# A new order of all operations, after the list scheduler's costs for the first products and the first loads are changed

## The chip, the cores and the metric

The kernel runs on one core of one Trainium2 chip. The metric is the device time of one execution in microseconds. The core has five engines with a queue of instructions each: TensorE (PE, matrix products), VectorE (DVE), ScalarE (ACT), GpSimd (POOL) and SyncE (SP), which here issues the transfers (DMA). An engine takes its instructions in the order in which the program lists them and waits where an input or a buffer isn't ready.

## The reference

The input `u` has 2 sequences of 2048 rows of 512 numbers. One block of a network is computed, with two parts.

- The mixer: `u @ W_in^T` gives z (1024 columns), xBC (1152) and 8 step sizes. xBC goes through a causal convolution of length 4 and `silu`, and is split into x (8 heads of 128), B and C (64 each). A state space scan follows for each head: within a chunk a masked product of C, B and decay factors with x, across chunks a carried state. The result is gated with `silu(z)`, normalised by its root mean square and multiplied with `W_out^T`. `u` is added, and each row is normalised to mean 0 and variance 1.
- The feed-forward part: the three weights are rounded to -1, 0, 1 times their mean magnitude. `hidden = silu(x @ wu^T) * (x @ wg^T)` has 2048 columns, and `hidden @ wd^T` is added to x; each row is normalised again.

## The kernel before

**Tiling.** The mixer works through 16 groups `g` of 256 rows, each of two chunks `c` of 128. The feed-forward part works through 8 blocks `b` of 512 rows. It computes its products by a scheme with seven instead of eight (P1 to P7 of `pair` and `down`), in 8 pairs `p` of blocks of hidden columns.

**Precision.** Operands of the large products are split into a high and a low float16 part. So weights are scaled first: `wsplit` loads a piece of a weight, squares and sums it on ACT (`sq`), sums over the partitions with a product (`mm`), takes a root on GpSimd (`pw`), and then writes the high part (`hi`, ACT) and the low part (`lo`, DVE). The window of `u` that a group needs goes the same way in `proj`: `ul` (L657) loads it, `usq` squares it, `usmm` sums, then come `uh` (ACT, L730 to L732) and `ulo` (DVE, L733).

**Names of steps.** In `proj`, `z{c}{j}` are products for z (L757), `x{j}` products for xBC (L774), each 12 instructions; `xt{j}` transposes (L789). `steps` makes the decay factors, `scan` the chunk's products (`yo`, `st`, `yd`) and the output products `o0` to `o2` (L974). In `pair`, `FP1.3` is product P1 of pair 3 (L1087); in `down`, `FQP20` is product P2 for one half of the rows (L1139), and `FRc11` and the like (L1149) add its bank to the residual. After the last `down` come row statistics, a root on GpSimd, the scaling and the output (L1235 to L1254).

**The order.** The program is not written in the order in which it runs. Each step is recorded as an operation with an engine, a cost in microseconds, the tiles it reads and writes and, for a transfer, its size `kb`. Then `Order.run` (L417) plays a list scheduler: it advances a clock, and whenever an engine is free it starts the operation with the lowest key whose inputs are done and whose buffers can be had. Buffers are handed out in the same pass. The resulting sequence is the program, and the time of the scheduler's clock is used for nothing else. The keys are the table `KEYS` (L41), one number for each of the 6287 operations in the order of their recording, in tenths of a microsecond; a small number is urgent. In the scheduler, a transfer ends `kb * 1.024 / BW` after the transfer before it or after its own start, with `BW = 290.0` (L368).

**The head.** The kernel's first loads are weights for `wsplit` (L645), the first window of `u` (L657) and the output weight in 8 pieces, twice (L685 and L702). While they come, PE has 80 groups of 4 products of a constant that nobody reads (L710 to L714, `WARM = 80`). They stand in the same list with keys of their own, and so are put between the real products.

```python
        for n in range(WARM):
            def idle():
                for i in range(4):
                    T.matmul(warm[:, :P * 2], oh[:, :P], oh, start=True, stop=True)
            op("", "PE", 4 * 0.109, idle, w=[warm], lat=0.0)
```

Of the kernel before, what the change touches and what calls it, by code (L numbers as in the profile page):

```python
# [41 lines left out]
69 16 66 80 87 90 97 100 115 245 279 287 327 330 338 340 348 165 176 219 233 273 283 290 292 314 46 89 100 114 123  # L42
131 134 152 112 155 166 188 191 198 201 212 136 179 191 207 217 224 229 241 191 240 276 283 302 309 313 358 305 355
383 403 479 532 548 563 347 392 192 263 272 514 530 748 759 773 798 725 753 765 771 226 260 299 333 337 371 361 395
238 272 292 326 351 385 220 254 406 412 895 929 936 782 817 826 944 978 990 863 897 915 923 957 984 902 936 976 998
1045 1071 788 822 838 24 28 32 37 41 46 50 54 59 63 67 72 76 83 87 92 96 103 107 112 116 120 127 131 136 140 145 149
153 158 162 169 173 207 212 216 220 225 229 236 254 272 279 283 307 312 316 334 338 343 350 354 374 379 401 408 412
436 441 445 450 492 496 503 534 546 550 554 561 603 608 645 650 681 693 697 701 706 743 748 113 125 132 135 142 144
164 259 750 820 343 374 397 194 265 278 417 473 470 290 345 350 482 484 541 502 509 515 520 522 524 526 528 530 533
536 542 546 555 562 579 592 662 595 636 680 691 660 621 664 672 649 361 381 393 399 404 440 444 448 539 547 385 402  # L50
408 437 453 543 559 597 507 530 537 543 551 636 643 686 194 215 229 237 253 368 399 426 178 196 208 225 233 285 358
378 320 346 354 375 380 493 500 534 240 267 274 279 285 392 434 485 476 499 505 510 515 594 601 639 258 288 300 305
310 481 490 496 872 924 821 852 726 753 841 866 303 347 379 390 398 429 441 868 486 531 626 660 662 458 503 488 663
700 834 1011 903 787 846 793 800 811 821 825 833 844 847 858 865 872 879 890 897 902 904 922 924 968 1003 1052 1062
1032 993 1044 1037 1021 521 539 547 556 579 669 677 664 690 721 565 602 610 615 621 717 724 746 772 810 816 821 834
908 929 991 612 631 639 644 649 742 752 782 654 681 687 700 705 802 810 831 668 696 710 715 720 768 786 805 759 788
794 801 812 872 889 921 710 748 755 761 767 828 838 882 858 885 891 898 904 988 1010 1066 931 963 584 606 909 942
949 984 454 534 724 781 787 797 859 738 805 812 952 727 775 788 958 967 983 987 994 1008 1021 1070 1053 1079 1114
1204 1357 541 560 845 944 946 966 873 866 891 1114 880 998 1012 1101 848 1004 1070 1107 1123 1138 1147 1155 1167
1230 1271 1211 1254 1315 1399 1500 911 926 934 937 944 947 964 1043 1010 997 1021 1060 1118 993 1015 1016 1070 1077  # L60
1266 1106 1225 1385 1412 1388 1390 1392 1394 1396 1398 1400 1402 1404 1406 1408 1410 1412 1414 1417 1424 1457 1524
1466 1505 1554 1564 1510 1491 1534 1546 1534 1145 1176 1182 1187 1192 1230 1280 1276 1251 1265 1101 1133 1139 1149
1160 1184 1195 1247 1173 1190 1196 1212 1222 1261 1271 1292 1333 1359 1366 1372 1377 1382 1387 1435 1237 1276 1286
1291 1296 1342 1346 1363 979 1005 1011 1017 1033 1069 1096 1149 1302 1330 1336 1351 1361 1366 1371 1379 1198 1220
1226 1242 1259 1289 1300 1339 1039 1072 1085 1090 1096 1151 1158 1187 1585 1627 1664 1684 1547 1583 1730 1766 686
751 1138 1113 1124 1132 1153 1143 1160 1263 1164 1176 1187 1279 1200 1216 1229 1305 1320 1335 1341 1348 1362 1433
1446 1406 1458 1491 1560 1868 754 895 1300 1258 1273 1287 1447 1462 1533 1623 1340 1355 1362 1478 1315 1329 1348
1472 1486 1498 1501 1508 1521 1748 1761 1567 1628 1806 1915 2034 1086 1098 1191 1203 1211 1234 1246 1733 1414 1290
1511 1562 1569 1389 1422 1423 1572 1574 1675 1650 1771 1604 1621 1620 1622 1634 1636 1652 1657 1673 1680 1686 1694
1701 1716 1721 1736 1743 1748 1787 1786 1873 1927 1978 1970 1952 1907 1950 1988 1963 1478 1519 1525 1530 1542 1553  # L70
1640 1627 1565 1762 1792 1822 1828 1833 1839 1974 2004 2027 1602 1631 1637 1653 1658 1805 1836 1933 1694 1716 1722
1737 1744 1930 1940 1993 1373 1412 1418 1424 1429 1438 1442 1471 1444 1481 1488 1493 1499 1504 1508 1541 1429 1446
1453 1459 1468 1538 1545 1557 1273 1295 1301 1311 1325 1442 1475 1501 1650 1689 1695 1702 1717 1763 1770 1819 1753
1786 1772 1826 1879 1936 1838 1873 1528 1634 1600 1657 1674 1681 1603 1609 1616 1811 1662 1687 1721 1798 1641 1680
1712 1792 1808 1838 1855 1862 1878 1936 1986 1923 1973 2034 2076 2332 1357 1415 1693 1791 1804 1823 1929 1996 2006
2052 1726 1862 1870 1958 1706 1889 1896 1964 1982 2002 2005 2013 2039 2264 2277 2083 2244 2322 2375 2471 1776 1790
1810 1820 1827 1831 1843 1999 1935 1876 1956 1986 1978 1905 1948 1950 1995 2003 2267 2035 2226 2297 2368 2304 2311
2313 2315 2318 2320 2325 2330 2339 2344 2360 2367 2369 2371 2373 2377 2390 2459 2396 2429 2481 2488 2458 2422 2473
2465 2447 1942 1995 2003 2008 2013 2023 2103 2107 2052 2111 1856 1879 1885 1895 1900 2000 2032 2040 2125 2144 2150
2155 2160 2363 2399 2415 1990 2030 2038 2043 2048 2108 2114 2256 2277 2314 2321 2326 2331 2348 2352 2395 2019 2068  # L80
2074 2079 2085 2241 2261 2286 2101 2121 2128 2138 2143 2298 2306 2345 2057 2082 2089 2103 2113 2283 2290 2301 2339
2370 2377 2382 2392 2435 2467 2483 2567 2608 2165 2207 2148 2183 2195 2221 1646 1699 2084 2047 2063 2070 2170 2176
2183 2251 2093 2107 2116 2233 2117 2132 2139 2239 2304 2316 2318 2326 2337 2400 2434 2382 2450 2489 2513 2821 1708
1741 2291 2232 2245 2264 2416 2422 2435 2576 2293 2305 2313 2428 2349 2361 2368 2434 2441 2454 2456 2464 2476 2560
2636 2520 2550 2681 2864 2975 2042 2054 2168 2178 2186 2188 2200 2574 2231 2230 2227 2262 2263 2402 2457 2457 2460
2498 2705 2581 2598 2665 2765 2676 2681 2715 2717 2729 2736 2748 2755 2758 2760 2762 2764 2766 2771 2776 2782 2811
2846 2815 2860 2903 2911 2870 2840 2883 2891 2881 2650 2680 2686 2694 2710 2806 2838 2834 2822 2862 2213 2258 2277
2282 2287 2367 2419 2439 2616 2666 2677 2682 2690 2859 2869 2884 2292 2321 2335 2340 2345 2432 2447 2461 2421 2452
2461 2496 2502 2591 2598 2606 2585 2613 2624 2634 2644 2671 2679 2803 2355 2380 2386 2396 2412 2480 2487 2594 2474
2533 2539 2544 2552 2646 2663 2674 2507 2542 2548 2556 2572 2603 2614 2659 2765 2799 2924 3000 2729 2756 2698 2723  # L90
2308 2374 2522 2587 2590 2601 2530 2524 2538 2648 2606 2628 2641 2781 2596 2617 2632 2658 2788 2805 2807 2815 2826
2862 2896 2871 2906 2941 3018 3232 2469 2588 2716 2623 2638 2666 2847 2840 2856 2969 2737 2748 2756 2825 2718 2730
2747 2819 2935 2947 2950 2957 2980 3157 3171 3025 3127 3216 3271 3355 2618 2629 2671 2674 2681 2686 2698 3025 2808
2758 2805 2835 2832 2787 2817 2810 2874 2921 2984 2971 2976 3094 3204 3115 3169 3174 3180 3187 3189 3191 3194 3197
3199 3201 3203 3205 3207 3209 3211 3251 3290 3254 3280 3335 3323 3319 3301 3346 3358 3330 2891 2931 2943 2948 2953
2993 3009 3004 3004 3052 2958 3005 3012 3018 3028 3038 3056 3088 3099 3143 3149 3170 3175 3283 3304 3364 3042 3064
3073 3079 3089 3109 3125 3210 3007 3042 3048 3054 3069 3090 3096 3117 2716 2761 2767 2772 2777 2881 2888 2900 2838
2873 2879 2899 2918 2968 2989 2997 2825 2847 2853 2858 2875 2897 2904 2981 3083 3113 3123 3133 3153 3213 3233 3256
3180 3221 3488 3547 3371 3408 3337 3380 2852 2981 2952 2980 2984 2991 2963 2957 2972 3093 3001 3032 3071 3181 2990
# [416 lines left out]
def mamba_ffn_kernel(  # L516
# [5 lines left out]
    nc = tc.nc  # L522
# [43 lines left out]
    with ExitStack() as ph:  # L566
# [4 lines left out]
        op = od.op  # L571
# [71 lines left out]
        def wsplit(nm, part, slot, src, dst, lo, n, tag):  # L643
            st = mk(tag, [P, n])
# [10 lines left out]
        def load_u(g):  # L655
            raw = uraws[g] = mk("uraw", [P, 4, TW])
            op("ul", "SP", 0.5, lambda: nc.sync.dma_start(out=raw.ap, in_=uT[g]), w=[raw], kb=520)  # L657
# [25 lines left out]
        for n in range(8):  # L683
            raw = mk("fraw", [P, DM])
# [15 lines left out]
        for n in range(8):  # L700
            raw = mk("fraw", [P, DM])
# [601 lines left out]
```

## Time and profile before

| what | us |
|---|---|
| median of 3 runs | 1363.52 (1363.44 to 1363.9) |
| the profiled execution | 1363.4 |
| its span, first to last instruction | 1361.7 |
| TensorE busy with products | 1347.8 |
| VectorE, ScalarE, GpSimd busy | 1162.3, 1067.4, 85.3 |
| first product begins, last one ends | 1.1, 1354.0 |

The profile is of one execution. Its span is 1.7 us shorter than the time of that execution. A product's end is modelled: products are pipelined, so in a run of products each is shown longer than the distance to the next. Mixer work fills the stretch from the start to about 800 us, feed-forward work what follows; the head is the part with unread products, up to 77 us. In the rows of waits the columns are the waiting engine with its tile and line, what it waited for, the total in us, the times, and the longest.

### The profile page before, as it was taken

The numbers are of one execution on the slowest core, as the hardware profiler recorded it, in microseconds if no ns is written. First come the engines' busy times: TensorE is split into PE (matmuls) and PEld (weight loads), VectorE is DVE, ScalarE is ACT, GpSimd is POOL, SyncE is SP. The second block draws the span as 40 slices with busy tenths as digits, with TensorE's granted clock in tenths as the row PEclk, the third lists the DMA queues.
The fourth block names the chain that finished last, engine by engine and source line by source line (L and its number), as shares of the span: only waits on it lengthen the run. The fifth ranks groups of instructions, "written<-read, shape, count | busy, mean of one in ns | idle before, by whom it ended". The sixth has DMA issues, their size and how long they took to land.

```text
span 1361.7 us, 29015 instructions
## 1 busy us (share of the span) xinstructions
PE 1347.8 (99%) x11046; PEld 1061.1 (78%) x11046; DVE 1162.3 (85%) x3111; ACT 1067.4 (78%) x2015; POOL 85.3 (6%) x128
## 2 busy tenths in 40 slices
PE   9999999999999999999999999999999999999997
PEld 8877676666767676776666688888888888888886
DVE  5789869988988889999998787988979697979885
ACT  7888878787877878879877785969788686969663
POOL 1000000000000000000000100001010101010000
PEclk9999999999999999999999999999999999999999
DMA  6434553564525625446559721313232232322001
GB/s 219 142 95 124 146 142 97 160 170 132 147 57 140 173 63 148 141 141 158 124 139 218 191 52 26 92 40 102 48 91 50 86 55 94 48 85 49 24 17 47
DMA packets 194811, 145.60 MB, mean 107 GB/s; under 512 B 140656, under 2 KB 151920, under 8 KB 194672
## 3 DMA queue, kind: packets, MB, share of 16 engines
q1 hardware_dynamic: 194672, 143.75, 40.3%
q8 instruction: 86, 1.41, 0.4%
q14 instruction: 53, 0.43, 0.1%
HBM read 89.84 MB, written 22.41 MB: 82 GB/s over the span
## 4 chain that ended last, share of the span: by engine, by line
PE 74%; DVE 13%; ACT 8%; DMA 4%; issue 1%; POOL 0%; SPq 0%; POOLq 0%; ACTq 0%; DVEq 0%
PE sd L1087 13%; PE mm L757 8%; PE po L974 8%; PE mm L774 7%; PE sd L1139 6%; PE po L1087 5%; PE mm L1087 5%; DVE acc L781 3%; PE ms L1087 3%; PE po L1139 3%; PE sd L954 3%; PE mm L1139 3%; PE tr L1087 2%; PE tr L789 1%; PE sd L917 1%
## 5 line engine op out<-in xcount | busy, mean ns | idle before, releaser
L781 DVE SCALAR_TENSOR_TENSOR acc<-mm,cwu,acc 128x256 f32<-128x256 f32 x432 | 202.7, 481 | 21.0 <-ACT acc L779 18.5
L1087 PEld LDWEIGHTS <-wx 128*128 128x128 fp8e4 x2048 | 200.3, 98 | 24.2
L774 PEld LDWEIGHTS <-wx 128*128 128x128 f16 x1728 | 165.6, 97 | 36.7 <-issue 3.6
L1087 PEld LDWEIGHTS <-wz 128*128 128x128 fp8e4 x1536 | 150.3, 98 | 18.2
L774 PE MATMUL mm<-uh,wx 128*128 128x260 f16 x1152 | 152.4, 274 | 1.6 <-DVE v L762 0.7
L757 PE MATMUL mm<-wz,uh 128*128 128x344 f16 x768 | 127.7, 309 | 1.1 <-ACT sz L764 0.5
L974 PE MATMUL po<-wo,th 128*128 128x512 f16 x512 | 121.1, 379 | 0.1
L779 ACT ACTIVATE acc<-mm,cst,cwu 128x256 f32<-128x256 f32 x144 | 80.1, 557 | 34.0 <-PE mm L774 33.6
L757 PEld LDWEIGHTS <-uh 128*128 128x128 f16 x768 | 74.0, 98 | 39.0 <-issue 3.8
L974 PEld LDWEIGHTS <-th 128*128 128x128 f16 x512 | 48.8, 98 | 49.7 <-issue 0.8
L774 PE MATMUL mm<-ul,wx 128*128 128x260 f16 x576 | 87.6, 273 | 0.0
L785 ACT ACTIVATE xc<-acc 128x256 f32<-128x256 f32 x128 | 52.6, 413 | 29.3 <-DVE acc L781 28.4
L757 PE MATMUL mm<-wz,ul 128*128 128x344 f16 x384 | 71.7, 309 | 0.0
L947 DVE SCALAR_TENSOR_TENSOR cr<-cr,dt,gm 128x128 f32<-128x128 f32 x256 | 71.4, 347 | 0.2
L764 ACT ACTIVATE sz<-mm,szs 128x344 f32<-128x344 f32 (+1 forms) x96 | 51.3, 538 | 21.3 <-PE mm L757 20.0
L954 PE MATMUL sd<-xt,cr 128*128 128x128 f32 x512 | 67.5, 278 | 0.0
L954 PEld LDWEIGHTS sd<-xt,cr 128*128 128x128 f32 x512 | 62.2, 192 | 3.3 <-DVE rr L834 0.4
L974 PE MATMUL po<-wo,tl 128*128 128x512 f16 x256 | 60.5, 379 | 0.0
L865 DVE TENSOR_SCALAR cr<-cr,cum 128x128 f32<-128x128 f32 x256 | 54.0, 282 | 5.2 <-DMA cr<-cum_scratch 5.2
L791 ACT ACTIVATE xt<-tr 128x256 f32<-128x256 f32 x128 | 48.1, 375 | 12.4 <-PE tr L789 12.3
L1139 PEld LDWEIGHTS <-xt 128*128 128x128 f16 x512 | 50.0, 98 | 7.2 <-DVE xt L1122 1.2
L757 PEld LDWEIGHTS <-ul 128*128 128x128 f16 x384 | 37.6, 98 | 18.4
(319 smaller groups left out, 3294.2 us busy)
## 6 DMA issues: line engine op xcount, KB each, us to landing
cr<-cum_scratch SPq DMA_DIRECT2D x32, 512.0 KB, 5.2
uraw<-in_uT_dram SPq DMA_DIRECT2D x16, 520.0 KB, 3.6
ec<-cum_scratch SPq DMA_DIRECT2D x64, 128.0 KB, 5.5
fraw<-in_wupT_dram SPq DMA_DIRECT2D x32, 256.0 KB, 3.4
s_scratch<-js SPq DMA_DIRECT2D x32, 256.0 KB, 2.7
x<-s_scratch SPq DMA_DIRECT2D x32, 256.0 KB, 3.0
fraw<-in_wgateT_dram SPq DMA_DIRECT2D x32, 256.0 KB, 3.5
fraw<-in_wdownT_dram SPq DMA_DIRECT2D x32, 256.0 KB, 3.0
```

What stands on the lines that cost most here:

```text
L757: T.matmul(ps[:, :ZC], (uh, ul)[a][:, k, HL + c * P:HL + (c + 1) * P], wz4[b]()[:, j, k, :], start=(n == 0), stop=(n == 11))
L764: op(f"sz{c}{j}", "S", act(w, 1), lambda: S.activation(d["sz"][c][:, j * ZC:j * ZC + w], ps[:, :w], AF.Silu, scale=szs[:, j:j + 1]), r=[ps ...
L774: T.matmul(ps[:, :TW], wx4[a]()[:, j, k, :], (uh, ul)[b][:, k, :], start=(n == 0), stop=(n == 11))
L779: op(f"t{j}3", "S", act(TG, 2), lambda: S.activation(acc.ap, ps[:, HL:TW], AF.Identity, bias=cb[:, j:j + 1], scale=cwu[:, j, 3:4]), r=[ps, ...
L781: op(f"t{j}{k}", "V", stt(TG), lambda k=k: V.scalar_tensor_tensor(acc.ap, ps[:, 1 + k:1 + k + TG], cwu[:, j, k:k + 1], acc.ap, ALU.mult, A ...
L785: op(f"xs{j}", "S", silu(TG), lambda: S.activation(xc.ap, acc.ap, AF.Silu), r=[acc], w=[xc], table="silu")
L865: V.tensor_scalar(cr[:, h, :], cr[:, h, :], cum[:, c * NH + h:c * NH + h + 1], 0.0, ALU.subtract, ALU.min)
L947: V.scalar_tensor_tensor(cr[:, h, :], cr[:, h, :], dt[:, c, h:h + 1], gm.ap, ALU.mult, ALU.mult)
L954: T.matmul(yp[hf][:, i * P:(i + 1) * P], cr[:, h, :], xt[:, c, h, :], start=is_first(g, c), stop=(is_first(g, c) or i == 3))
L974: T.matmul(po.ap, t[:, k, :], wo3[b]()[:, k, :], start=(q == 0 and k == 0), stop=(q == 2 and k == 7))
L1087: T.matmul(bank_[:, fi * TG:(fi + 1) * TG], wt[:, kt, f * P:(f + 1) * P], xT[i][:, a, :, kt, :], start=(first and fi == 0 and n == 0), sto ...
L1139: T.matmul(bank_[:, s_ * TG:(s_ + 1) * TG], X[k][j][:, a, e, s_ * P:(s_ + 1) * P], wt[:, k, :], start=(first and s_ == 0 and k == 0 and a ...
```

## The change

Five costs that the list scheduler uses are changed, and all 6287 keys. The instructions of the program are the same; their order on every queue, SP's and GpSimd's among them, and the choice of buffers follow from the new keys and costs.

- The transfers of the weight pieces, of the first window of `u` and of the output weight count as 0.72 of their former size (`n` columns of 128 rows of 4 bytes are n / 2 KB).
- The first 6 of the 80 groups of unread products count 0.213 us for each product instead of 0.109.

```diff
 KEYS = """
-69 16 66 80 87 90 97 100 115 245 279 287 327 330 338 340 348 165 176 219 233 273 283 290 292 314 46 89 100 114 123
...
-13492 13503 13508 13528 13474 13484 13499 13497 13504 13515 13533
+57 2 44 59 85 99 106 109 123 184 218 225 247 272 280 285 295 179 103 141 154 165 167 175 178 190 -6 32 43 56 63 71
...
-            op(nm + "ld", "SP", 0.5, lambda: nc.sync.dma_start(out=st.ap, in_=src[:, lo:lo + n]), w=[st], kb=n / 2)
+            op(nm + "ld", "SP", 0.5, lambda: nc.sync.dma_start(out=st.ap, in_=src[:, lo:lo + n]), w=[st], kb=0.36 * n)
...
-            op("ul", "SP", 0.5, lambda: nc.sync.dma_start(out=raw.ap, in_=uT[g]), w=[raw], kb=520)
+            op("ul", "SP", 0.5, lambda: nc.sync.dma_start(out=raw.ap, in_=uT[g]), w=[raw], kb=520 if g else 374)
...
-            op(f"wa{n}ld", "SP", 0.5, lambda n=n, raw=raw: nc.sync.dma_start(out=raw.ap, in_=woT[:, n, :]), w=[raw], kb=256)
+            op(f"wa{n}ld", "SP", 0.5, lambda n=n, raw=raw: nc.sync.dma_start(out=raw.ap, in_=woT[:, n, :]), w=[raw], kb=184)
...
-            op(f"wb{n}ld", "SP", 0.5, lambda n=n, raw=raw: nc.sync.dma_start(out=raw.ap, in_=woT[:, n, :]), w=[raw], kb=256)
+            op(f"wb{n}ld", "SP", 0.5, lambda n=n, raw=raw: nc.sync.dma_start(out=raw.ap, in_=woT[:, n, :]), w=[raw], kb=184)
...
-            op("", "PE", 4 * 0.109, idle, w=[warm], lat=0.0)
+            op("", "PE", 4 * (0.213 if n < 6 else 0.109), idle, w=[warm], lat=0.0)
```

The first number of the table is the key of the first load of `u`, and the second that of the load of wz2. The numbers of the 80 groups of unread products go from 2.4 to 74.8 us before, and from -2.3 to 93.0 after. The first loads by their new numbers are wx2 (-2.2), wx1 (-0.6), wz2 (0.2), wx3 (3.2), u (5.7), wx0 (10.3), wz1 (10.8), the constants (17.9), wx8 (18.4) and wz0 (25.9); before they were wz2 (1.6), wx1 (4.6), u (6.9), wx2 (11.2), wx3 (13.6), the constants (16.5), wx0 (17.6), wz0 (19.1), wx8 (24.5) and wz1 (30.5).

## The prediction

> **What bounds the kernel now.** I read the page first, for the share of each engine; then the busy times by stretch; then the waits of TensorE alone; then the head and the end of the timeline.
>
> ```profile
> span 1361.7 us, 29015 instructions
> PE 1347.8 (99%) x11046; PEld 1061.1 (78%) x11046; DVE 1162.3 (85%) x3111; ACT 1067.4 (78%) x2015; POOL 85.3 (6%) x128
> ```
>
> TensorE is the bound: 1361.7 - 1347.8 = 13.9 us of the span are not covered by a product. The stretches (columns: length, then busy us of PE, PEld, DVE, ACT, POOL, the granted clock, DMA share, GB/s) say where:
>
> ```profile
> 0.00:100.00 100.00, 98.22 (x810) 78.79 (x811) 72.67 (x228) 83.16 (x156) 8.07 (x20) 1.00 0.46 150
> 100.00:775.00 675.00, 671.61 (x4964) 466.40 (x4963) 596.14 (x1862) 542.88 (x1021) 36.49 (x52) 1.00 0.54 140
> 775.00:1300.00 525.00, 525.00 (x4796) 469.04 (x4795) 450.24 (x923) 407.69 (x777) 36.39 (x48) 1.00 0.26 64
> 1300.00:1354.00 54.00, 52.96 (x483) 46.87 (x480) 39.84 (x88) 32.27 (x59) 3.25 (x6) 1.00 0.06 20
> ```
>
> The head lacks 1.8 us (1.1 before the first product, 0.65 in small gaps), the mixer 3.4, the feed-forward part nothing, the last blocks 1.0; the rest is the 7.7 us after the last product, which ends at 1354.0. What PE waited for in 100 to 775, and in the last stretch:
>
> ```profile
> PE mm L774 <- DVE v L762: 0.7, 2, 0.6
> PE mm L757 <- ACT sz L764: 0.5, 2, 0.4
> PE tr L789 <- ACT xt L791: 0.5, 2, 0.3
> ...
> PE po L1139 <- DVE xt L1122: 1.0, 1, 1.0
> ```
>
> These are single stalls of 0.3 to 0.6 us, each with another cause, and one of 1.0 us: the first product of the last `down` waits for the last pieces of `pair`. No line repeats, so no one edit removes them; a new order draws them anew.
>
> **The change part by part.** No instruction is added or removed. Every PE instruction is the same, so the PE work is the same 1347.8 us less what overlaps, and the time can move only by idle PE time and by the end after the last product.
>
> *The two corrected costs.* They alter what the list scheduler believes, and nothing on the chip by themselves.
>
> ```profile
> 1.12 5.50 PE L713 MATMUL po<-ones 128*128 128x256 f16 x25 [1.12 <-DVE magic L562]
> 6.00 3.24 PE L713 MATMUL po<-ones 128*128 128x256 f16 x26
> ...
> 19.57 1.06 PE L774 MATMUL mm<-uh,wx 128*128 128x260 f16 x8
> ...
> GB/s 0 0 0 121 22 110 385 396 418 407 410 421 424 432 418 418 402 434 391 409 401 432 391 451 385 339 389 385 397 410 327 122 210 343 418 324 231 224 21 0
> ```
>
> The first 25 unread products (L713) take 5.50 us, less a drain of about 0.16 (one is shown with a median of 272 ns, though in a run the next starts about 110 ns later): 0.213 us each. The next 26 take 3.24, less the drain: 0.118, the first of them still slow. The new cost, 0.213 for the first 6 groups of 4, fits this row: 6 x 4 x 0.104 = 2.5 us that the old list did not count. The chip pays them before and after: 0. Here a rule weighs against the change: the Trainium skill, "TensorE: Matmul & The Clock Gate", Part 1 (What's actually happening), gives the slow start as about 3.4 us of time in a free-running window and says not to fit a specific count of products. By it 3.4 / 0.213 = 16 products are slow, and the list is wrong by 8 x 0.104 = 0.8 us at the head, which shifts real products against their loads. The row decides: 24 to 25 products, one execution. The 0.8 goes into the range.
>
> The DMA rates of the first 20 us (half a us each) stand at 385 to 432 once the stream runs, about 406. A piece of 512 KB (524,288 bytes) takes 1.29 us; the old list says 512 x 1.024 / 290 = 1.81, the new one 368.6 x 1.024 / 290 = 1.30. The other rule: the skill's "DMA: Bandwidth & Descriptors", section Where 436 GB/s comes from, sets about 358 GB/s for reads from HBM. By it a piece takes 1.46, and the eight loads that stand first in the new table (four of 512, two of 688, one of 520, one of 39 KB: 3983 KB) end at 11.4 instead of 10.0 us of streaming, 1.4 late, and PE stands for up to that. The row says 406, so I cost it at 0.
>
> *The new places at the head.* SP's queue: before, the window of u came third (wz2, wx1, u, wx2, ...). By the new numbers SP issues wx2, wx1, wz2, wx3, then u. ACT's wait for the first load, 688 KB, ended at 5.15; at 406 GB/s that is 1.74 us of streaming, so the stream begins at 3.4. Before, u landed at 3.4 + 1.74 + 1.29 + 1.31 = 7.7; now it lands at 3.4 + 3 x 1.29 + 1.74 + 1.31 = 10.3. Behind it stand square, `usmm`, root, `uh`, `ulo`. The first real product began at 19.57, and the timeline shows its `ul` (L733) ending only at 19.3; with u later, it begins at about 22.3. The cover is the unread products: 35 groups stood before the first real one, now 39 (their numbers below that of x4). Four groups are 1.7 us and the small products some more. PE stays busy, and this costs nothing; 41 groups are left for later holes instead of 45. If the cover were gone, it would be the 2.6. The five and later weight loads move behind u too; GpSimd's roots follow the squares, one at a time, 0.55 us each, and keep their distance. The gaps within the head sum to 0.65; loads that the list knows can save some of it, and a list without slack can lose 0.8 to 1.4. I take -0.2, bounds -0.65 to +1.4.
>
> *The table.* All 6287 numbers are new: half differ by over 5.4 us, one in ten by over 22.6; in the mixer (100 to 775) half differ by over 7.8, in the feed-forward part by over 4.1. They are tenths of a microsecond, so a table can be laid out as a timetable: sort PE's operations by number, and call a hole what lies between one operation's number plus its cost and the next number. I take no time from it, only where this order has nothing for PE. Before: 2.4 us of holes, 2.0 of them behind 1315. New: 7.8 us: 4.0 in the feed-forward part (2.16 at 844 ahead of FP1.3, 0.86 at 925, 0.73 at 997, the rest small) and 3.8 behind 1315 (1.23 ahead of FP4.7, 0.93 ahead of the last block's P1). The chip prices them: the old 2.0 at the end became the one stall of 1.0 in the fence above, the old 0.39 in 775 to 1300 became none (525.00 of 525.00). So the end: 3.8 x 0.5 = 1.9, +0.9 (bounds 0 and 3.8 - 2.0 = +1.8). The middle: at 0 if other ready products fill the holes, since the scheduler never leaves PE idle while one is ready (FQP31 and FP2.2 stand near 844), +3.65 if none does; a hole of 2.16 is five times what vanished before, so I take half, +1.8.
>
> *The mixer's draw.* Its 3.4 us are stalls that the old list did not foresee. The new order shares its costs and draws them again; it cannot save over 3.4, and it can lose more: bounds -2.5 and +4, and I take +0.8, their middle.
>
> *The end.* Last stay P31 and P30, then residual, statistics, root, output: 7.7 us. FRc11 now comes later (P20 stands just ahead of P31), but DVE's 0.48 us pieces fit beneath P31 and P30 (3.5 us). 0.
>
> Sum: -0.2 + 0.9 + 1.8 + 0.8 = +3.3. The profiled execution took 1363.4 (span 1361.7 and 1.7 around it): **1366.7**, against the median of 1363.52 slower by 0.23%. 0.2%, 2.7 us, is about what a measurement of this kernel can tell from no change.
>
> **Rivals.** *It changes nothing:* the holes in the middle are filled, the draw is even, the end costs its 0.9: 1363.4 + 0.9 = 1364.3. For: the same PE work, and DVE at 450 of 525 in the feed-forward part leaves room. Against: the new table's holes. *Faster:* one mechanism, the mixer's order of DVE and ACT: if the list now hands PE its inputs before it asks, the stalls of 100 to 775 fall from 3.4 to 0.4 with nothing lost elsewhere: 1363.4 - 3.0 = 1360.4. It decides only if 2.8 of the 5.0 us of stalls go. Against: the corrected costs end with the first 60 us, and these stalls lie behind them. *DVE as a second bound in the mixer:* it is busy 596 of 675 there; if the new order lets one chunk's `scan` chain come 0.3 us late in each of the 16 groups, that is 16 x 0.3 = 4.8, with the end +0.9 and the middle +1.8: 1370.9. For: 88% leaves 79 us of slack for 32 chunks, and the table moved most there. Against: PE has only 11 named waits there now, 2.8 us in all.
>
> **How the numbers follow.** The likeliest, holes kept in part: 0.43, its own range 1364.6 to 1369; of it 0.28 lies beyond +0.2%. No change 0.21. Faster 0.17. DVE 0.19, all slower. Slower: 0.28 + 0.19 = 0.47; same: 0.15 + 0.21 = 0.36; faster 0.17. The range reaches into both outer cases and leaves out half of each, 0.18 in all: 1360.3, which is also 1363.4 less the lower bounds of head and mixer together (3.15), to 1371.0; the upper bounds of all parts at once (10.9) would be 1374.3.
>
> **What would show it.** PE's sum within 1 us of 1347.8, and the end at 7.7 +- 0.3: that only idle time moved. Head: the first real product at about 22, with over 35 groups before it; PE at 98 us or more of the first 100. Middle: PE at 523 of 525 in 775 to 1300; if it is 525 again, the holes were filled. End: a stall of 1.5 to 2 us ahead of the last `down`. Mixer: PE waits of 3 to 5 us in 100 to 775. The prediction is wrong if the mixer's waits halve, or if one wait, repeated for each group, tops the list.

## The result and the profile after

| | before | after |
|---|---|---|
| median | 1363.66 us (1363.44 to 1363.9, 6 runs) | 1372.03 us (1370.75 to 1374.04, 6 runs) |
| ratio | | 1.0064, interval 1.0054 to 1.0073 |
| profiled execution, its span | 1363.4, 1361.7 | 1371.81, 1370.1 |

The new order is slower by 8.4 us. The forecast was +3.3 us, so its sign was right, and its size was too small by more than half; 1372.0 lies above the upper end of its range, 1371.0. The page of the changed kernel, first lines:

```profile
span 1370.1 us, 29022 instructions
PE 1348.6 (98%) x11046; PEld 1062.3 (78%) x11046; DVE 1165.5 (85%) x3111; ACT 1055.6 (77%) x2005; POOL 85.7 (6%) x128
```

PE does as many products as before and is busy 0.85 us longer. The other 7.5 us are idle time. DVE has the same number of instructions; ACT has 10 fewer and is 11.8 us less busy, since the new order needs 52 loads of a function table instead of 62. So what is computed is the same, but ACT's table loads are not, and the kernel is slower although ACT has less to do. The stretches of the changed kernel (columns as before) say where it lies:

```profile
0.00:100.00 100.00, 95.31 (x778) 75.72 (x780) 71.91 (x227) 80.44 (x152) 9.27 (x20) 1.00 0.44 144
100.00:775.00 675.00, 667.22 (x4934) 464.67 (x4935) 595.28 (x1856) 530.81 (x1010) 35.62 (x52) 1.00 0.53 140
775.00:1300.00 525.00, 524.38 (x4777) 467.25 (x4776) 447.86 (x915) 406.52 (x776) 36.34 (x48) 1.00 0.26 66
1300.00:1362.00 62.00, 61.34 (x561) 54.61 (x560) 47.04 (x100) 36.03 (x67) 3.39 (x6) 1.00 0.05 18
```

Set against the same stretches of before, the head lost 98.22 - 95.31 = 2.9 us, the mixer 671.61 - 667.22 = 4.4, the feed-forward part 0.6; the last blocks idle for 0.7 instead of 1.0, which is -0.4 with the unrounded numbers; the tail is 7.7 us in both. 2.9 + 4.4 + 0.6 - 0.4 and the 0.85 of longer busy time make 8.4, all of the difference of the spans.

The waits of PE over the whole span (waiting engine, tile and line, what it waited for, us in total, times, the longest):

```profile
PE mm L774 <- DVE acc L781: 3.2, 3, 1.9
PE po L974 <- DMA th<-yh: 1.8, 1, 1.8
PE mm L757 <- DVE acc L781: 1.7, 2, 1.0
PE mm L774 <- ACT sz L764: 1.3, 3, 0.5
...
PE po L1139 <- DVE xt L1122: 0.7, 1, 0.7
```

The reader is to see two single stalls of nearly 2 us, which the old order had not. Its longest were 1.1 at the start and 1.0 at the end. The timeline of PE around the first of them (start, length, engine, line, what, number; in brackets the idle time before it):

```profile
593.32 1.34 PE L757 MATMUL mm<-wz,uh 128*128 128x344 f16 x8
594.50 0.75 PE L757 MATMUL mm<-wz,ul 128*128 128x344 f16 x4
597.41 1.05 PE L774 MATMUL mm<-uh,wx 128*128 128x260 f16 x8 [1.95 <-DVE acc L781]
...
599.00 2.50 PE L757 MATMUL mm<-wz,uh 128*128 128x344 f16 x8
601.29 1.05 PE L757 MATMUL mm<-wz,ul 128*128 128x344 f16 x4
```

The 12 products at 593.32 take until 595.25, 1.93 us. The same 12 at 599.00, behind the stall, take until 602.34, 3.34 us. The row of the granted clock over these stretches says why (the last three columns are the clock, the DMA share and GB/s):

```profile
595.00:598.00 3.00, 1.05 (x10) 0.80 (x9) 3.00 (x11) 1.94 (x4) 0.00 (x0) 1.00 0.72 238
598.00:602.00 4.00, 4.00 (x20) 2.34 (x18) 4.00 (x13) 1.99 (x3) 0.00 (x0) 0.57 0.05 20
```

From 598.5 to 601.9 TensorE ran at half its clock. That is 1.4 us for these 12 products and 1.7 us for the whole 3.4 us. So this stall costs 1.95 + 1.7 us, and the second part of it counts as busy time.

Who was late at 597? The timeline of DVE shows it standing just before, with `ulo` (L733) and the adds of the convolution, which free the bank of products, queued behind it:

```profile
591.93 1.66 DVE L865 TENSOR_SCALAR cr<-cr,cum 128x128 f32<-128x128 f32 x8 [2.33 <-DMA cr<-cum_scratch]
```

That transfer was issued at 584.95 behind three loads of 256 KB (the raw feed-forward weights, `fraw`, L1015) and landed at 591.90, after 7.0 us; the list scheduler had counted 4.7. At the second stall, at 755.7, a transfer is late too. SP's queue:

```profile
746.96 3.00 SPq L1066 DMA_DIRECT2D wz<-wq_scratch  x6
750.08 2.38 SPq L965 DMA_TRANSPOSE th<-yh  x1
```

The transposing transfer of `yh` to `th` stands behind six loads of rounded weights (L1066) and, in the chain of waits, takes 7.44 us; the median of the 32 such transfers is 3.2 to its landing. Here the list scheduler knows of the six loads: it has 7.2 us for this transfer. What it does not have is the lateness of SP's queue. SP issues the transfer 10.9 us behind the scheduler's clock, when PE is 9.1 us behind it, and the list leaves only 0.3 us between the landing and the product that needs it.

For the head, the timeline of ACT:

```profile
28.02 1.28 ACT L785 ACT_TABLE_LOAD   x1
29.31 0.42 ACT L785 ACTIVATE xc<-acc 128x256 f32<-128x256 f32 x1
...
35.75 1.28 ACT L676 ACT_TABLE_LOAD   x1
37.04 0.21 ACT L676 ACTIVATE negA<-cst 128x8 f32<-128x8 f32 x1
37.27 1.28 ACT L764 ACT_TABLE_LOAD   x1
```

The first `silu` needs a table that is not loaded yet: 1.28 us. The scheduler takes this one as there from the start (`table = "silu"`) and counts nothing for it. The two loads that follow, for `negA` (an exponential) and back, it does count. Before, `negA` stood ahead of the first `silu`:

```profile
17.82 0.19 ACT L676 ACTIVATE negA<-cst 128x8 f32<-128x8 f32 x1
...
27.88 1.28 ACT L785 ACT_TABLE_LOAD   x1
```

The chip made one load here, and the old list counted two, for `negA` at 14.3 us and for the `silu` at 24.4 of its own clock. So the old list has one load too many in the head and the new one has one too few. Before, PE's only wait in 20 to 100 us was one of 0.3.

**One more view: lateness.** `Order.run` ends with a time for each operation on its own clock, its plan. I took, for every operation, its start in the trace less its start in the plan. PE's lateness along the plan, in us (of before, 2.5 are taken off all values: the slow first products that its plan did not count):

| at plan time | 20 | 90 | 500 | 620 | 780 | 1300 |
|---|---|---|---|---|---|---|
| before | 0.6 | 1.2 | 1.3 | 2.7 | 3.1 | 3.9 |
| after | 0.9 | 5.3 | 5.4 | 8.4 | 10.9 | 12.7 |

Three things follow. The plans are as long as each other: that of before ends at 1352.1, that of after at 1354.6, which is the 2.5 us now counted; PE idles 2.4 us in both, all but 0.1 of it at the end. The 7.8 us of holes that I read from the table of keys are not in the order that the scheduler makes of it. So all of the loss is chip against plan. And it comes in few steps: more than before by 3.8 us in 20 to 90, by 1.6 in 500 to 620, by 2.1 in 620 to 780 and by 1.0 in the feed-forward part.

### The profile page after: what moved, and what is told of

Its sections match the earlier page's. It is cut to its first block, busy times and chain, and to the rows that moved or that the text cites. A ratio compares the mean times of both kernels' runs of the same rounds, so it can differ in the third digit from the quotient of the medians.

```text
span 1370.1 us, 29022 instructions
## 1 busy us (share of the span) xinstructions
PE 1348.6 (98%) x11046; PEld 1062.3 (78%) x11046; DVE 1165.5 (85%) x3111; ACT 1055.6 (77%) x2005; POOL 85.7 (6%) x128
## 4 chain that ended last, share of the span: by engine, by line
PE 64%; DVE 16%; ACT 11%; DMA 4%; issue 3%; POOL 1%; SPq 0%; POOLq 0%; ACTq 0%; DVEq 0%
PE sd L1087 12%; PE mm L774 7%; PE sd L1139 6%; PE po L974 6%; PE mm L757 6%; PE po L1087 5%; PE mm L1087 5%; DVE acc L781 4%; PE po L1139 3%; PE mm L1139 3%; PE ms L1087 2%; PE sd L954 2%; DVE cr L947 2%; PE tr L1087 2%; DMA cr<-cum_scratch 1%
## 5 line engine op out<-in xcount | busy, mean ns | idle before, releaser
L1087 PEld LDWEIGHTS <-wx 128*128 128x128 fp8e4 x2048 | 200.4, 98 | 24.4
```

The lines of the kernel that those rows point to most:

```text
L1087: T.matmul(bank_[:, fi * TG:(fi + 1) * TG], wt[:, kt, f * P:(f + 1) * P], xT[i][:, a, :, kt, :], start=(first and fi == 0 and n == 0), sto ...
```

## The experiments

The theory after these traces, called the margin theory: by counting 2.5 us too little at its head, the old plan ran ahead of the chip. Every input planned for a moment had 2.5 us more, and what the plan doesn't count (the table load, late transfers) was hidden. For the table load this cannot hold as it stands, since the old plan counts it. The new plan is right at the start and has nothing to pay with. The rival: the loss lies in single places of the new order, in the head and in the transfers that stand behind loads, whatever the margin is. The kernel before ran beside all of them (medians 1363.6 to 1364.6), and each is given as a ratio to it, with its interval (it is not the quotient of the two medians).

### More and fewer unread products

`a_lead24` gives the new order 24 more unread products at its start, 2.6 us that its plan doesn't count.

```diff
-            def idle():
-                for i in range(4):
+            def idle(n=n):
+                for i in range(28 if n == 0 else 4):
```

> The new kernel with 24 unread products more in the first group (28 instead of 4), not told to the list: the same order on every queue, 24 x 0.109 = 2.6 us more work for PE at the very start. Margin theory (the old list left PE 2.5 us behind its own plan, so that ACT, DVE and the loads ran ahead; the new list is exact and PE now pays for each thing that the list does not know): the stalls of the first 85 us, about 4 us, give most of the 2.6 back, and the time is 1371.5 to 1372.8, at most 0.8 above the new kernel's 1372.0. Queue theory (only late transfers behind other transfers in SP's queue, at 585 and 750 us, cost time): nothing is given back, 1374.6.

1373.27 us, ratio 1.0061 (1.0048 to 1.0074): 2.6 us more work, and no change beside the new order's 1.0064. The time is that of the margin theory, but the trace speaks against its reason. PE's lateness still rises by 4.3 us between 20 and 90 (4.4 without the extra products), with the same stalls in the first 100 us as in the new order itself:

```profile
PE mm L774 <- ACT sz L764: 1.2, 2, 0.7
...
PE mm L757 <- DVE acc L781: 1.0, 1, 1.0
PE mm L774 <- DVE acc L781: 0.9, 1, 0.9
```

The 2.6 went elsewhere. Lateness at 20 is 1.8 instead of 0.9, so 1.7 of them are gone by then: the clock rose at 3.85 us instead of 4.56, and PE waited less. And this execution had no stretch of half clock at 597.

`b_less24` takes the same 24 products out of the old order (`range(0 if n < 6 else 4)`).

> The kernel before with the first 6 groups of unread products emitted empty (24 products fewer; the list still counts them): the same order, 2.6 us less work for PE. Margin theory: PE loses the lag of 2.5 us against its plan, and stalls in the first 100 us take back a good part: 1361.6 to 1363.4. If the lag covers nothing: 1363.6 - 2.6 = 1361.0.

1365.63 us, ratio 1.0008 (0.9999 to 1.0016). Work of 2.6 us less gains nothing, and the time lies above what either theory expected. But the head keeps: PE is at 98.24 of the first 100, lateness 1.1 at 90. The loss comes later, in three steps: +0.9 at 253, +2.0 at 548, +1.7 at 738. The last two in the waits of PE:

```profile
PE po L974 <- DMA th<-yh: 2.3, 2, 1.5
PE mm L774 <- DVE acc L781: 2.1, 2, 1.7
```

So a lag of 2.5 us is worth something to the old order, but not at the head, and what pays for it are waits of the same two names as in the new order.

### The table load alone

One `silu` of one column, before everything else, brings the `silu` table with the load at 0.80 us that every run has, where ACT has nothing to do.

```diff
     V.memset(half, 0.5)
+    first = const.tile([P, 1], F32, name="first")
+    S.activation(first, half, AF.Silu)
```

> The new kernel with one silu of a single column on ACT ahead of the first load, so that the silu table is there from the start and the table load at 28 us (1.28 us, not in the list's costs) goes. Margin theory: ACT and DVE are 1.4 us less late from 29 us on, the stall of PE at 32.7 (1.0 us) goes and PE's lateness at 85 us falls by 0.7 to 1.2; the time falls by 0.3 to 1.1, to 1371.0 to 1371.7. Queue theory: the head does not matter for the end, the stalls at 595 and 755 stay where their transfers put them: 1371.8 to 1372.2.

1373.39 us in the median of executions from 1369.57 to 1373.7, ratio 1.0053 (1.0040 to 1.0066): at most a little faster than the new order. Its stretches and waits say more. The first 100 us:

```profile
0.00:100.00 100.00, 97.91 (x807) 78.22 (x808) 74.65 (x231) 82.19 (x157) 9.24 (x20) 1.00 0.46 152
```

PE has 97.91 of 100 instead of 95.31, lateness at 90 is 2.3 instead of 5.3. That is one pair of executions. Of the ten kernels here with the new order, the five with the early `silu` have PE at 97.06 to 97.91 of the first 100 us, the five without it at 95.31 to 96.97: 1.6 us on average. What goes in all five is PE's wait of 0.96 us at 33 us. The waits at 74 and 76 us (0.87 and 0.52), behind a transfer `cr` of 7.28 us, come back in part in four of them. But the lateness of `a_silu` at 1300 is 11.6, against 12.7. What was won is mostly lost again at 551 (+1.0), 595 (+2.3) and 755 (+1.9, and then half clock until 759.0). Its longest waits are those two places:

```profile
PE mm L776 <- DVE acc L783: 2.1, 1, 2.1
PE po L976 <- DMA th<-yh: 2.0, 1, 2.0
```

> The kernel before with the same early silu. Margin theory: there PE is 3.6 us behind its plan when the table is loaded, so the 1.28 us of ACT are covered already: no change, 1363.4 to 1363.8. If the table load is paid in full by PE in any order: 1362.4.

The old order with the same edit (`b_silu`): 1364.33 us, ratio 0.9998 (0.9989 to 1.0006). But the edit does something else here. `negA` stands ahead of the first `silu` in this order, so the early table is replaced at once, and the load before the first `silu` stays:

```profile
16.99 1.28 ACT L678 ACT_TABLE_LOAD   x1
...
27.05 1.28 ACT L787 ACT_TABLE_LOAD   x1
```

So the run shows that one load more, at 17 us, costs the old order nothing. What one load less would be worth there was not tried.

### Moving the loads in front of the late transfers

The finished sequence was edited: named operations are taken out and put behind another one.

```diff
-        for o in self.run():
+        for o in self.moved(self.run()):
```

`a_wlate` puts the six weight loads behind the late transfer `th` and two more of the same group. `a_crfirst` puts the three loads of `fraw` behind the transfer `cr` that was late. `a_all` does both, with the early `silu`.

> The new kernel with one edit in SP's queue: the six loads W50, W60, W20, W51, W61, W21 (256 KB each, not needed before 768 us) are issued behind th.1, tl.1 and ss.0 of group 14 instead of ahead of them. Late-transfer theory: PE's wait of 1.7 to 2.1 us for th.1 at 755 us goes and nothing behind it is limited by anything but PE: the time falls by 1.5 to 2.2, to about 1370. Rival (the new order has no slack anywhere, and a stall taken away comes back at the next place): within 0.6 of 1372.0.

1370.94 us, 1.0059 (1.0045 to 1.0073). The stall at 757 is gone, and a new one stands 8 us later, on the next group's transfer, which now is the one behind the loads:

```profile
PE po L984 <- DMA th<-yh: 1.3, 1, 1.3
```

> The new kernel with one edit in SP's queue: three loads of 256 KB (up weights, not needed before ACT reaches them) go behind cr0 and cr1 of group 12 instead of ahead of them. Late-transfer theory: DVE's wait of 2.3 us for cr0 at 590 us goes, and with it PE's stall of 2.1 us at 595 and the 3.4 us at half clock that followed it in the profiled run (1.4 us): PE's lateness does not jump at 597 to 602, and the time falls by 2 to 3.5, to 1368.5 to 1370. Rival (the stall comes back elsewhere): within 0.6 of 1372.0.

1373.74 us, 1.0078 (1.0064 to 1.0092), if anything slower than the new order. Now the three loads are late, ACT waits for them, and PE for ACT, with half clock from 589.4 to 592.8:

```profile
PE tr L799 <- ACT bt L814: 3.0, 1, 3.0
```

> The new kernel with the early silu, the six W loads behind th.1 and the three loads behind cr0 and cr1. If head (3.0 us in the profiled run with the early silu), 595 us (2.1 and 1.4 at half clock) and 755 us (1.7) add up, the time falls by about 8 to 1363.5 to 1366, the level of the kernel before. Rival (no slack, the loss moves on): 1369 or more.

1372.59 us, 1.0064 (1.0051 to 1.0076). The head is mended (lateness 3.6 at 90) and all of it lost at 589 (+3.2, and 1.6 of half clock), 767 (+1.6) and 871 to 876 (+1.7). Here moves within a full queue handed a stall on; they can't show what the stall is worth.

### Taking the load off the queue

So the next pair makes the loads light: a quarter of the bytes of `fraw` is read, in both orders. The rounding of the feed-forward weights then works on partly unread data; the number of transfers and of all other instructions is the same.

```diff
-... nc.sync.dma_start(out=raw.ap, in_=w_src[i][:, lo:lo + DM]) ...
+... nc.sync.dma_start(out=raw[:, :P], in_=w_src[i][:, lo:lo + P]) ...
```

> The new kernel with the second reading of the feed-forward weights cut to a quarter: each of the 48 pieces in ternary() loads 128 of its 512 columns (64 instead of 256 KB), the rest of the tile keeps what it held, so the rounded weights are not the reference's; every instruction and every queue is as it was. 9.4 MB of the 145.6 are not moved. Transfer theory (in 575 to 770 us cr0 and th.1 come late because loads stand ahead of them): the steps of PE's lateness at 597 and 757 go, with the half clock behind the first: 1366 to 1368.5. Rival (the order of DVE and ACT alone makes PE wait): 1371 or more.

1370.93 us, 1.0053 (1.0041 to 1.0065). The time is near what the rival expected, but the step at 597 is gone: lateness at 620 is 4.4 instead of 8.4. The stall at 755, whose six loads are not of `fraw`, stays and now draws half clock (755.4 to 758.8, 1.7 us):

```profile
PE po L974 <- DMA th<-yh: 2.2, 1, 2.2
```

> The kernel before with the same cut loads (64 instead of 256 KB for the 48 pieces of ternary(), the rest of the tile stale). Transfer theory: its list left room, so it gains little: 1362.3 to 1363.7, and the distance to the new kernel with the same cut falls from 8.4 to about 4.5. Rival: the distance stays 7 to 9.

1364.5 us, 1.0004 (0.9996 to 1.0012): the old order gains nothing from lighter loads. The distance of the two orders is 6.4 us with them, 8.4 without.

> The new kernel with the cut loads and the early silu. If head (3.0 us through the table load) and transfers are the two halves of the loss and no third thing takes their place: 1363 to 1365.5, within 2 us of the old kernel with the cut loads. Rival (lateness taken away at the head comes back behind 500 us in any case): the same as the new kernel with the cut loads alone, within 0.7.

1369.35 us (1365.88 to 1371.12), 1.0036 (1.0022 to 1.0049), between the two expectations. Alone, each edit gave 0.0011 of the time; together they give 0.0064 - 0.0036 = 0.0028, 3.8 us. Only the last is clear of the intervals: those of either edit alone overlap the new order's, so whether the two are worth more together than apart is not shown. Lateness in the profiled execution, one of the shortest with 1366.21, is 2.5 at 620 and 7.0 at 1300.

`a_sum` adds the third: the last three of the six weight loads move behind the transfers that were late.

> The new kernel with the early silu, the cut loads of ternary() (64 instead of 256 KB for 48 pieces, rest of the tile stale) and the three second halves W51, W61, W21 (needed from 789 us on) issued behind tl.0 of group 15, so that th.1 of group 14 stands behind three loads fewer. If head, transfers and the clock behind the stalls are the whole loss: the step at 752 to 757 us falls below 0.4, no 3.4 us at half clock, 1363.5 to 1366, runs close together. Rival (something else moves into its place): 1368 or more, like the new kernel with cut loads and early silu.

1366.3 us (1365.5 to 1368.09), 1.0020 (1.0013 to 1.0028). Lateness 3.5 at 90 and 6.1 at 1300, and no half clock after the start. The mixer's stretch and the longest wait:

```profile
100.00:775.00 675.00, 669.89 (x4957) 466.87 (x4956) 593.72 (x1855) 531.46 (x1012) 35.63 (x52) 1.00 0.50 126
```

```profile
PE mm L769 <- DVE acc L793: 1.4, 1, 1.4
```

The three causes together are 0.0064 - 0.0020 = 0.0044 of the time, some 6 of the 8.4 us (3.5 to 8 by the ends of the two intervals). 2.7 us remain, in stalls of up to 1.4; which property of the order makes them stays open. The choice of buffers, which changes with the order, was not varied by itself.

`a_mend` is the attempt to have this without leaving data out: the early `silu`, the three moved weight loads, and the last of the three `fraw` loads behind the first transfer `cr` of its pair.

> The new kernel with nothing left out: early silu, W51, W61, W21 behind tl.0 of group 15, and the third of the three loads at 583 us behind cr0 of group 12. By the sum of the parts: head -3.0, th.1 -1.5, half of the stall at 597 and its half clock -1.5: 1366 to 1368.5. If what is taken away comes back at the next transfer: 1370 or more.

1369.44 us (1367.9 to 1369.84), 1.0041 (1.0028 to 1.0054): better than the new order by about a third of its loss, though the two intervals touch, short of what was expected, and still slower than the old order. 1.6 us at 593 stay.

### The two halves of the change

`b_costs` keeps the old table of keys and takes the new costs; `b_keys` takes the new table with the old costs.

> The old table with the five new costs, the other half of the change alone: the list then makes another order (its own plan leaves PE 5.3 us idle instead of 2.4, 2.3 of it at 74 to 88 us). If the plan's idle time shows on the chip: 1363.7 + 2.9 = 1366 to 1367.5. If the costs matter only through the table: 1363.0 to 1364.5.

1371.21 us, 1.0051 (1.0038 to 1.0064), above both expectations. Its plan is itself worse (PE idles 5.3 us in it, and it ends at 1357.5), and the same transfer is late again:

```profile
PE po L974 <- DMA th<-yh: 2.1, 1, 2.1
```

> The new table with the five old costs, the other half of the change alone. The list then makes nearly the new order (14% of PE's places differ, with as little idle time in its plan, 2.5 us). If the loss belongs to the table and not to the costs: 1370 to 1374. If counting the head exactly makes the loss: 1363 to 1366.

1369.64 us, 1.0041 (1.0028 to 1.0054). Its plan is as good as the others (idle 2.5, end 1352.2), and it is still slower than before by 5.6 us. Here `negA` comes ahead of the first `silu`, ACT makes one table load in 20 to 45 us instead of three, and PE has 97.99 of the first 100 us: a head without the loss of the new order does not save the rest. Each half alone does most of the harm. That speaks against a price for correct costs as such: of the four combinations, only the old table with the old costs has no stall of PE over 1.1 us (the others have 1.4 to 2.1). Why that one escapes was not found out.

### Lag and light loads together

The last run asks whether the old order's lag covers the transfers: `b_less24` with light `fraw` loads.

> The kernel before with 24 unread products fewer and the cut loads of ternary() (64 instead of 256 KB for 48 pieces, rest of the tile stale). If the lag of 2.5 us at the head covered transfers in 540 to 740 us: the steps at 548 (2.0) and 738 (1.7) that the kernel with 24 fewer showed go, and the 2.6 us are kept: 1361.3 to 1362.8. If the lag covered ACT and DVE: 1363.8 to 1365.5.

1364.83 us (1361.97 to 1369.89), 1.0009 (1.0002 to 1.0015). The 2.6 us less work are not kept. In the profiled execution, one of the longer ones, two stalls are back at other places, 255 and 740, and the first is followed by half clock:

```profile
PE po L974 <- ACT xt L791: 2.4, 1, 2.4
PE po L974 <- DMA th<-yh: 2.2, 1, 2.2
```

```profile
255.00:259.00 4.00, 3.96 (x14) 1.41 (x16) 4.00 (x12) 3.97 (x8) 0.00 (x0) 0.57 0.85 246
```

The fastest of its executions, 1361.97, is below all 38 of the kernel before on that chip (1362.21 to 1365.59). A gap of 0.24 us does not show that the 2.6 us are to be had where such stalls stay away. The median lies in the range that was expected if the lag covers ACT and DVE, and of the two stalls in the trace one is a wait for ACT and one for a transfer. So what the lag covers in the old order was not shown.

## Why the prediction was wrong

Three steps failed. The head had no term for a table load that the new list leaves out. The holes read from the keys are not in the order that the scheduler makes. And the mixer's stalls were taken to be of the old size, with nothing for the half clock behind one. That the sign was right was luck: 2.7 of the forecast +3.3 us are the holes, and the loss came from elsewhere.

**What bounds the kernel: right.** PE's sum is within 1 us (1348.6), the last product to the end takes 7.7, and only idle PE time and clock moved the time. Two readings were inexact: ACT's instructions do change (10 fewer table loads), and PE's named waits in 100 to 775 were 10, not 11.

**The corrected costs: wrong on the count.** I let the row of one execution decide on 24 to 25 slow products, against the Trainium skill's page "TensorE: Matmul & The Clock Gate", Part 1 (What's actually happening). The timeline of the changed kernel's start:

```profile
1.12 4.46 PE L713 MATMUL po<-ones 128*128 128x256 f16 x24 [1.12 <-DVE magic L562]
```

24 products in 4.46 less the drain of 0.16 are, at 0.213 and 0.109 each, 16 slow ones and 8 fast ones: 16 x 0.213 = 3.4 us, what the page gives; the 25 of before were 5.3 us. In the profiled executions of all kernels the clock rose between 3.85 and 6.47 us. A row from one execution can't fix a number that changes with each; the page's warning was right. It saves 0.9 us of busy time in the changed kernel's profile and is not the cause of the loss.

**The new places at the head (-0.2, bounds -0.65 to +1.4): failed.** The first real product was forecast for 22.3, behind 39 groups of unread ones; it began at 22.12, behind 39 (156 products of L713). But PE was busy 95.31 of the first 100, not 98. I had priced the cover, unread products for as long as real ones are missing, and stopped at the first real product. The loss came behind it, from 33 to 77 us: PE waits for banks that ACT and DVE have to free, and ACT is late by a table load that the new list does not count. I had no term for a cost that the list leaves out: the old one counted a load too many in the head, the new one a load too few. Measured: +2.9 in the stretch, of which the early `silu` gives back 2.6 in one pair of executions and 1.6 on average.

**The table's holes (+1.8 in the middle, +0.9 at the end): failed.** The plan that the scheduler makes of the new table has no more idle time than that of before. The feed-forward part lost 0.6, and the stall ahead of the last `down` is 0.7, shorter than before's 1.0, where I had forecast 1.5 to 2. Keys say which operation is more urgent. I took them for a timetable, which the scheduler does not keep.

**The mixer's draw (+0.8, bounds -2.5 and +4): direction right, size wrong.** It lost 4.4, just beyond the upper bound. I reckoned with more stalls of the old size, 0.3 to 0.6 us. It was two of nearly 2 us (1.95 + 1.8 = 3.75 of the 4.4), each behind one transfer that queued behind loads of other work, and on top the clock: +1.7 of busy time after the first, of which the shorter slow start hides 0.9. Neither a stall of this size nor the half clock had a term in the sum.

**The rivals.** In time, DVE as a second bound came nearest (1370.9), but its mechanism is not there: no wait repeats from group to group, and DVE is busy 595 of 675 as before.

## What to carry to other kernels

Where one engine is busy 99% of the span, compare the plan's times with the trace operation by operation: what the plan has wrong (here a table load that it leaves out, a transfer that took 2.3 us longer than counted, and one that its queue issued late) shows as steps in one engine's lateness, and an order can be spared such a cost without anyone having planned it. Removing one of several such causes moved little here, since the next late input took the time; only runs that removed two or three at once stood clear of the noise. And urgency numbers tell nothing of idle time: run the scheduler and read the plan it makes.

## What the hardware showed that was not expected

- One idle stretch of about 2 us of TensorE can be followed by 3.4 us at half clock, which is 1.7 us of work: after 1.95 us in the changed kernel, 2.02 in `a_silu` (at 755), 2.16 in `a_light`, 2.38 in `b_less24_light`, 3.0 in `a_crfirst`, 3.1 in `a_all`. Its length alone does not decide: 2.10 us in `b_costs`, 2.14 in `a_silu` (at 595), 2.21 in `b_less24_light` (at 740) and 2.59 in `a_lead24` were not followed by it. The same section of the Trainium skill's page on TensorE sets an idle window of about 3.4 us for that; here a shorter stretch was enough in these six cases.
- It differs between executions of one kernel. Those of the changed kernel with a mean clock of 0.999 took 1370.75 to 1372.26, those with 0.996 and 0.997 1371.81 to 1374.04.
- The same transfer of `yh` to `th` took 3.0 us to 7.7 us to land, and the 7.4 us one stood behind six weight loads on its queue. PE is listed as waiting for one of the 32 only, that one.
